# Decoder layer in fp32: a shared product behind the gates, and weight chunks summed on GpSimd ahead of their means

## Chip, core and metric

The kernel runs on one core of a Trainium2 chip. The metric is device time in microseconds (us) of one execution. The texts call the engines by their names and the profile by its short forms: TensorE is PE (PEld is its weight load), VectorE is DVE, ScalarE is ACT, GpSimd is POOL, and SP issues the DMA transfers. A line number such as L997 is a line of the kernel before.

## What is computed

The input x has 16 sequences of 256 tokens of 512 features, all in fp32. Three parts follow each other, each with a residual and a layer norm:

```python
x = _layernorm(x + _L0_attn_ref(x, ...))        # gated state space block
x = _layernorm(x + _L0_xattn_ref(x, k, fside_S2_0, ctx_2048, ctx_2048, 8))
x = _layernorm(x + _L0_ffn_ref(x, W, b, lora_A, lora_B, gate_w, gate_b))
```

The first part projects x to z, xi, dt, B and C, convolves xi over four tokens, scans 16 states per head, and projects back. The second is a long convolution: the 256 rows of each half of the batch are taken as 32 heads of 8 rows; `kv` is the product of every row of v with every row of x2 in a head, it is convolved along the 512 features with the causal kernel of the head, `skip` times `kv` is added, and the result is multiplied with x1 and summed over the rows:

```python
kv = vr[:, :, :, None, :] * x2r[:, :, None, :, :]
y = irfft(rfft(kv, n=2 * L) * rfft(k, n=2 * L)[None, :, None, None, :], n=2 * L)[..., :L]
y = y + kv * skip
out = einsum('bhijl,bhil->bhjl', y, x1r)
```

The third is a feed-forward layer with eight low-rank experts, of which the two with the highest gate values are taken:

```python
base = x_flat @ W.T + b
logits = x_flat @ gate_w.T + gate_b
topk_logits, topk_idx = jax.lax.top_k(logits, 2)
gates = jax.nn.softmax(topk_logits, axis=-1)
out = base + lora_update          # gates times lora_B of lora_A of x_flat, for the two experts
```

## The kernel before

The order of instructions is written out by hand: inside `manual_schedule` every engine runs its instructions in the order in which the program emits them, and the framework adds the waits for data and for buffers. A tile pool with `bufs=n` for a tag holds n tiles of that tag at once; the first write to a further tile waits until the last reader of an earlier one is done.

**Part 1** runs from 0 to about 760 us, in eight groups (`g`) of 512 tokens. A group has ten steps (`i`), each a pair of output channels of xi (`x`), z, B or C. A step emits `first_products` (16 matmuls), then `last_products` of the step before (12 matmuls), then the sums of both on VectorE and ScalarE, and for an `x` step the convolution over tokens in `mixed`: channel 2p begins on VectorE (L575), channel 2p + 1 on ScalarE (L573), and three L577 on VectorE follow for each. These results are tiles of the tag `acc`, of which there are six:

```python
acc = p2.tile([P, GB, S], F32, tag="acc", name="acc", bufs=6)
```

`head_means(0)`, at step 6, reads the accumulators of channels 0 to 3, and `head_means(1)`, at step 8, those of channels 4 to 7. Both write `xm` (L588), a PSUM tile of the tag `tr`, of which there are two. The order of a group from the second on is x0, z0, x1, x2, z1, x3, b0, c1, z2, z3; at step i the sums of step i - 1 are finished, so channels 0 and 1 are mixed at step 1, 2 and 3 at step 3, 4 and 5 at step 4, 6 and 7 at step 6.

In group 1 (105.1 to 201.6 us) the weights of part 3 are prepared beside that. At step 2 `with_identity` adds the residual to `w_f` (L518, L520). At step 5 `centred` takes the mean of `w_f` over its 512 rows and subtracts it, at step 6 that of `w_gl`. The mean is a matmul with `share`, a matrix of 1/512, accumulated over the four chunks of 128 rows (L526) into a tile `mw` of the tag `tr`; the subtraction is four VectorE instructions (L530).

**Part 2 and part 3** run together from about 750 us to the end, one head `h` of 32 after the other. A head's `kv` has two halves `q` of 512 columns. Each half goes through `seeded` (L997, L999), `convolve` (L1010 for whole blocks, L1025 for quadrants of the diagonal), and `contract`: `multiplied` (L1060, tile `pr`) and `reduced` (L1070). Two matrices of the convolution's block rows 2 and 3 share a product with the sum of two input blocks. `seeded` makes it once in the PSUM bank of row 3 and ScalarE copies it, with its two half-partitions exchanged, into the bank of row 2; the later matmuls accumulate onto it. The PSUM tiles `y` (two of two banks) have one buffer each, so the product of the second half waits for the first half's `multiplied`, which reads the same banks.

Between the halves TensorE does part 3 of the head before, which is why `ff` is false in head 0: `centre` transposes `o_l` (L1097) and runs the norm's statistics on ScalarE (L1170, L1088) and GpSimd (L1083, L1090, L1091), with `meanwhile` emitted between mean and squares; then come the eight matmuls of the gates and low-rank rows (`gl`, L1262) and three of the four feed-forward blocks (`base`, L1185). The fourth block, the gates' transposition and `lora` come in the first half of the next head. `gates` (L1104 to L1124) is a run of small VectorE instructions on [128, 8] to [128, 8, 8]. GpSimd also makes `t` (L934), `o` (L948, L952), the pair sums `xs` (L981), the differences `Td` (L986) and the skip products `sk` (L917) for the next head. VectorE makes the next head's `kv` in `products` (L155).

After `base`, `store` scales the finished rows on ScalarE (L1147) and sends them to memory through SP.

Of the kernel before, what the change touches and what calls it, by code (L numbers as in the profile page):

```python
# [8 lines left out]
F32 = mybir.dt.float32  # L9
AF = mybir.ActivationFunctionType  # L10
ALU = mybir.AluOpType
# [3 lines left out]
P = 128  # L15
B, S, D = 16, 256, 512
KD = D // P
# [14 lines left out]
NE, R = 8, 16  # L32
HP = P // 2
# [10 lines left out]
SHARED_AT, DIAGONAL_AT = 3, 5  # L44
# [8 lines left out]
ER = NE * R  # L53
# [17 lines left out]
def decoder_kernel(  # L71
# [24 lines left out]
    nc = tc.nc  # L96
# [83 lines left out]
    with ExitStack() as s1:  # L180
# [3 lines left out]
        p2 = s1.enter_context(tc.tile_pool(name="p2", bufs=2))  # L184
# [326 lines left out]
        def with_identity(w):  # L511

            for k, blk in enumerate(BLOCKS_OUT):
                own = w[:, k, blk * P : (blk + 1) * P]
                if blk in SWAPPED_OUT:
                    for a, b in ((0, HP), (HP, 0)):
                        half = own[:, a : a + HP]
                        nc.vector.tensor_tensor(half, half, ident[:, b : b + HP], ALU.add)  # L518
                else:
                    nc.vector.tensor_tensor(own, own, ident, ALU.add)  # L520

        def centred(w, cols):

            ps = ps_t.tile([P, 512], F32, tag="tr", name="mw")
            for kc in range(KD):
                nc.tensor.matmul(  # L526
                    ps[:, 0:cols], share, w[:, kc, :], start=(kc == 0), stop=(kc == KD - 1)
                )
            for kc in range(KD):
                nc.vector.tensor_tensor(w[:, kc, :], w[:, kc, :], ps[:, 0:cols], ALU.subtract)  # L530

# [6 lines left out]
                nc.sync.dma_start(first[sh][bi], r)  # L538

        heads = {}  # L540
        late = []
        for g in range(NG):
            xs = xs_next
            more = g + 1 < NG
# [95 lines left out]
            for i, (kind, p) in enumerate(order):  # L640
                if g == 1 and i == 2:
                    with_identity(w_f)
                if g == 1 and i in (5, 6):
                    centred(*((w_f, D), (w_gl, NE + ER))[i - 5])
                if i == 6:
                    ms = [head_means(0)]
                if g == 0 and i == 0:
                    al, be = first_products(
                        kinds[kind], p, True, None,
                        lambda: begun.append(begin_products(w_xi, order[1][1], False)),  # L650
                    )
                else:
                    al, be = first_products(
                        kinds[kind], p, i % 3 == 0, begun.pop(0) if begun else None
                    )
                if i == 8:
                    ms.append(head_means(1))
                if i == 9:


                    yps = ps_t.tile([P, S], F32, tag="tr", name="yps")
                    for ht in range(HT):
                        for b in range(GB):
                            nc.tensor.matmul(
                                yps[b * HP : (b + 1) * HP],
                                sel[:, ht].rearrange("p q h -> p (q h)"),
                                Bs[ht][:, b * S : (b + 1) * S],
                                start=(ht == 0),
                                stop=(ht == HT - 1),
                            )  # L670
                if before is not None:
                    finish_products()
                to = places(kind, p)
                u = first_sums(al, be, to)
                if i == 8:
                    states(1, stepped(ms[1], spreads[2]), spreads[3])
                if i == 6:
                    ms = [stepped(ms[0], spreads[0])]
                    spreads.append(spread(1, 1))
                if g == 0:  # L680
                    if i == 1:
                        parts = decays()
                    if i == 2:
                        nc.scalar.activation(A, A, AF.Exp)
                        nc.vector.tensor_scalar(A, A, -1.0, None, ALU.mult)
                    if i in (1, 2, 4):
                        next(parts)
                if i == 9:
                    yT = q3.tile([P, S], F32, tag="vn", name="yT", bufs=1)
                    nc.scalar.copy(yT, yps)  # L690
                if before is not None:
                    finish_sums((lambda: next(parts)) if g == 0 and i == 2 else None)
                if g == 0 and i == 3:
                    next(parts)
                if g == 0 and i in later:
                    for n, (w, k) in enumerate(later[i]):
                        ins = weight_sums(nc.gpsimd, w, k)
                        if n == 0:
                            wait_for(ins, mixes[-1])
                if i == 7:  # L700
                    states(0, ms[0], spreads[1])
                if i == 8:
                    outputs(0)
                    outputs(1)
                    if more:
                        rt = to_dram(rms(xs_next))
                    if g == 0:
                        behind = []
                        w_sums = w_o_sums(behind)
                        next(w_sums)  # L710
                before = (kind, p, al, be, u, to)
                if i < 2 and late:
                    normalised(g - 1, late.pop(0))
                if i == 1 and more:
                    xs_next = load_x(g + 1)
# [95 lines left out]
            late = []  # L811
            if more:
# [36 lines left out]
                late = [(1, xs[1]), (3, xs[3])]  # L849
            else:  # L850
                finish_sums()
                gated(1, spread_heads(1))
                for n, t in enumerate((0, 2, 1, 3)):


                    ps = ps_s.tile([P, 512], F32, tag="s", name="s") if n in (0, 3) else bank()
# [44 lines left out]
    with ExitStack() as s2:  # L901
# [64 lines left out]
        def bank_of(y, lb):  # L966
            n = BLOCKS_OUT.index(lb)
            return y[2] if len(y) > 2 and lb == 2 else y[n // 2][:, n % 2, :]
# [23 lines left out]
        def seeded(y, T, xs, q):  # L992

            yc = bank_of(y, 3)
            nc.tensor.matmul(yc, T[:, SHARED_AT, :], xs[:, q], start=True, stop=True)  # L997
            for a, b in ((0, HP), (HP, 0)):
                nc.scalar.copy(bank_of(y, 2)[b : b + HP], yc[a : a + HP])  # L999

        def convolve(y, kv, T, Td, q, between=None, late=False, early=None, ahead=None):

# [142 lines left out]
        def store(h, x3, nb, rs):  # L1145
            res = p2.tile([P, D], F32, tag="res", name="res")
            nc.scalar.activation(res, x3, AF.Identity, bias=nb, scale=rs)  # L1147
            nc.sync.dma_start(out[h * P : (h + 1) * P, :], res)
# [34 lines left out]
        def feed_forward(base, o_l, kcs, first=False):  # L1183
            for kc in kcs:
                nc.tensor.matmul(  # L1185
                    base, o_l[:, kc, :], w_f[:, kc, :], start=(first and kc == kcs[0]), stop=False
                )

        last, done, rest = None, None, None
        for h in range(HX):  # L1190
# [8 lines left out]
            if h:  # L1199
                if nxt:  # L1200
                    v_after = turned_v(vns.pop(0), ps_b, "vp")
                    kvs.append(load_T(h + 1))
                    if h + 2 < HX:
                        vns.append(load_v(h + 2))
                        cTs.append(load_c(h + 2))
                if rest is not None:
                    base, o_r, xa = rest
                    feed_forward(base, o_r, (3,))
                    turned = turned_gates(xa)
                seeded(y, T, xs, 0)  # L1210
                if rest is not None:
                    lora(base, [turned])
            if ff:
# [34 lines left out]

            def meanwhile():
                skips.append(skip_term(cT, ws, behind))  # L1250
                if nxt:
                    seeded(y, T, xs, 1)

            if ff:
                rs = centre(o_l, meanwhile)
# [3 lines left out]
            if ff:  # L1259
                gl = ps_t.tile([P, NE + ER], F32, tag="tr", name="gl")  # L1260
                for kc in range(KD):
                    nc.tensor.matmul(  # L1262
                        gl, o_l[:, kc, :], w_gl[:, kc, :], start=(kc == 0), stop=(kc == KD - 1)
                    )
                base = ps_b.tile([P, D], F32, tag="base", name="base")
                feed_forward(base, o_l, (0, 1, 2) if nxt else (0, 1, 2, 3), True)
            if ready is not None:
                store(*ready)
            if nxt:
                products(v_n, cT_n, kv_n, 1)  # L1270
                more_next = prepared(kv_n, T_n)
                more_next[2](0)
                more_next[3]()
                sk_next = skip_sums(h + 1, kv_n)
                more_next[2](1)
# [164 lines left out]
```

## Time and profile before

| | before |
|---|---|
| Median of 3 runs | 1461.5 us (1461.34 to 1461.96) |
| The profiled execution | 1461.27 us |
| Its span in the profile | 1459.5 us |
| TensorE busy | 1423.8 us |
| VectorE busy | 1185.4 us |
| ScalarE busy | 438.1 us |
| GpSimd busy | 462.4 us |
| Group 1 of part 1 | 105.10 to 201.64, 96.54 us |
| Groups 2 and 3 of part 1 | 91.96 us each |
| One head of part 2 | 21.6 us |

The span runs from the first instruction to the last, and the time of an execution holds some 1.8 us more. A busy time is the union of an engine's instructions; the ends of matmuls are modelled, so matmuls that follow each other closely overlap in the view, and the distance from start to start tells more than a duration. In a line of the page or of the timeline stand the start and the duration in us (timeline) or the busy time and mean duration (page), the engine, the line, the operation, what it writes and reads with partitions and elements, how often, and in brackets how long the engine had been idle and for whom. One fp32 product appears as two MATMUL records.

### The profile page before, as it was taken

How to read it: one execution, taken by the hardware profiler on the slowest of the kernel's cores; microseconds unless marked ns; L12 is line 12 of the kernel's file. 1: busy time of each engine (PE TensorE's matmuls, PEld its weight loads, DVE VectorE, ACT ScalarE, POOL GpSimd, SP SyncE). 2: the span in 40 equal slices, each digit the busy share in tenths (PEclk: the TensorE clock that was granted, in tenths of full speed). 3: DMA queues.
4: the chain of work that ended last, by engine and by line, in shares of the span. 5: the costliest groups of instructions: out<-in, count | busy, mean ns of one | idle time of the engine just before them, and what ended most of it. 6: DMA issues, size and time to landing. Idle time of an engine off the chain costs nothing.

```text
span 1459.5 us, 19028 instructions
## 1 busy us (share of the span) xinstructions
PE 1423.8 (98%) x6956; PEld 915.1 (63%) x6956; DVE 1185.4 (81%) x2102; ACT 438.1 (30%) x962; POOL 462.4 (32%) x655
## 2 busy tenths in 40 slices
PE   9999999999999999999999999999999999999997
PEld 7788888888888878888773444444443444444443
DVE  6988778787787877878758888888888888888886
ACT  3423223233233332332202232332332333233222
POOL 5450020100101001010015545545554554554552
PEclk9999999999999999999999999999999999999999
DMA  8013111121111212112022122122112212212200
GB/s 294 32 41 125 43 47 44 37 81 31 58 44 36 82 22 69 44 37 89 8 83 65 44 66 73 48 69 65 61 55 66 70 46 66 72 44 65 73 26 22
DMA packets 49166, 89.18 MB, mean 61 GB/s; under 512 B 8880, under 2 KB 13360, under 8 KB 49072
## 3 DMA queue, kind: packets, MB, share of 16 engines
q1 hardware_dynamic: 49072, 87.96, 19.0%
q8 instruction: 55, 0.90, 0.3%
q14 instruction: 39, 0.32, 0.1%
HBM read 70.62 MB, written 17.32 MB: 60 GB/s over the span
## 4 chain that ended last, share of the span: by engine, by line
PE 94%; DVE 4%; issue 1%; POOL 1%; DMA 0%; ACT 0%; POOLq 0%; SPq 0%; DVEq 0%; ACTq 0%
PE mm L328 20%; PE y L1010 15%; PE s L328 13%; PE y L1025 12%; PE base L1185 7%; PE s L768 6%; PE mm L768 6%; PE y L997 4%; DVE pr L1060 3%; PE gl L1262 2%; PE base L1181 2%; PE tr L145 1%; PE mm L725 1%; PE xm L588 1%; PE mm L859 1%
## 5 line engine op out<-in xcount | busy, mean ns | idle before, releaser
L1060 DVE TENSOR_TENSOR pr<-y,cT 128x1024 f32<-128x1024 f32 x126 | 148.5, 1219 | 103.1 <-PE y L1025 103.1
L1025 PE MATMUL y<-kv 64*64 64x512 f32 x1536 | 179.6, 598 | 0.0
L577 DVE SCALAR_TENSOR_TENSOR acc<-xi,wc,acc 128x512 f32<-128x512 f32 x192 | 141.9, 753 | 7.4 <-ACT acc L573 1.7
L1070 DVE TENSOR_REDUCE red<-pr 128x128 f32<-128x1024 f32 x126 | 147.1, 1209 | 0.0
L155 DVE TENSOR_TENSOR kv<-tr,cT 128x1024 f32<-128x1024 f32 x124 | 145.5, 1215 | 0.0
L1010 PE MATMUL y<-kv 128*128 128x512 f32 x272 | 128.2, 594 | 0.6 <-ACT y L999 0.4
L1025 PEld LDWEIGHTS y<-kv 64*64 64x64 f32 x1536 | 52.2, 132 | 119.0 <-issue 96.8
L1185 PE MATMUL base<-w_f,ol 128*128 128x512 f32 x248 | 116.5, 593 | 0.0
L1010 PE MATMUL y<-kv,Td 128*128 128x512 f32 x248 | 116.5, 592 | 0.0
L66 POOL TENSOR_TENSOR rs_a<-ve_a,nhalf 128x1 f32<-128x1 f32 x32 | 18.9, 592 | 242.4 <-DVE ve_a L64 242.4
L1010 PEld LDWEIGHTS y<-kv 128*128 128x128 f32 x272 | 51.1, 190 | 66.4 <-issue 48.9
L997 PE MATMUL y<-xs,kv 128*128 128x512 f32 x124 | 67.9, 629 | 24.5 <-DVE pr L1060 23.5
L389 POOL TENSOR_TENSOR rstd<-ms,nhalf 128x4 f32<-128x4 f32 (+1 forms) x9 | 8.5, 945 | 260.8 <-DVE ms L387 260.8
L328 PE MATMUL mm<-XT,w_z 128*128 128x256 f32 x384 | 90.7, 379 | 0.0
L999 ACT COPY y<-y 64x512 f32<-64x512 f32 x124 | 69.2, 558 | 65.1 <-PE y L997 63.1
L1010 PEld LDWEIGHTS y<-kv,Td 128*128 128x128 f32 x248 | 47.1, 190 | 59.3 <-issue 59.3
L1217 POOL TENSOR_TENSOR ol<-o,red 128x512 f32<-128x512 f32 x31 | 39.4, 1271 | 140.3 <-DVE red L1070 140.3
L981 POOL TENSOR_TENSOR xs<-kv 128x512 f32<-128x512 f32 x63 | 80.0, 1269 | 2.4
L328 PEld LDWEIGHTS mm<-XT,w_z 128*128 128x128 f32 x384 | 73.0, 190 | 9.9
L328 PE MATMUL mm<-xnT,w_z 128*128 128x256 f32 x288 | 71.0, 382 | 0.0
L1185 PEld LDWEIGHTS base<-w_f,ol 128*128 128x128 f32 x248 | 42.5, 190 | 30.9 <-issue 30.9
L328 PE MATMUL s<-XT,w_xi 128*128 128x256 f32 x256 | 61.0, 380 | 0.9 <-DVE XT L224 0.6
(276 smaller groups left out, 2790.9 us busy)
## 6 DMA issues: line engine op xcount, KB each, us to landing
cT<-in_ctxT SPq DMA_DIRECT2D x32, 384.0 KB
kv<-in_toep SPq DMA_DIRECT2D x32, 384.0 KB
xt<-in_x SPq DMA_DIRECT2D x32, 256.0 KB
spread<-both SPq DMA_DIRECT2D x32, 256.0 KB
first<-xt SPq DMA_DIRECT2D x32, 256.0 KB
vn<-first SPq DMA_DIRECT2D x32, 256.0 KB
out<-res SPq DMA_DIRECT2D x31, 256.0 KB
xnT<-in_xT SPq DMA_DIRECT2D x7, 1024.0 KB
```

The lines of the kernel that those rows point to most:

```text
L155: last = nc.vector.tensor_tensor(kv[:, q, k * BQ : (k + NL // 2) * BQ], vT[:, q, blks].rearrange("p k (b i) -> p (k b) i", i=NH).unsqueeze ...
L328: nc.tensor.matmul(ps, w[:, p, a, kc, :], Xs[b][:, kc, :], start=start and kc == 0, stop=stop and kc == 1, skip_group_check=upon,)
L577: ins = nc.vector.scalar_tensor_tensor(acc, xi[:, :, k : k + S], wc[:, c, k : k + 1], acc, ALU.mult, ALU.add)
L768: nc.tensor.matmul(ps, own[a][c][:, n * P : (n + 1) * P], w_o[b][c], start=start and c == 0, stop=stop and c == HC - 1, skip_group_check=upon,
L981: return nc.gpsimd.tensor_tensor(xs[:, q], moving(kv, q, 0), moving(kv, q, 1), ALU.add)
L997: nc.tensor.matmul(yc, T[:, SHARED_AT, :], xs[:, q], start=True, stop=True)
L999: nc.scalar.copy(bank_of(y, 2)[b : b + HP], yc[a : a + HP])
L1010: nc.tensor.matmul(bank_of(y, lb), w, moving(kv, q, mb), start=not late and lb not in begun, stop=False, skip_group_check=True,)
L1025: return nc.tensor.matmul(bank_of(y, lb)[cols], T[rows, DIAGONAL_AT, (b - a) * HP : (b - a + 1) * HP], moving(kv, q, lb)[rows], start=star ...
L1060: nc.vector.tensor_tensor(pr.rearrange("p (k b j) i -> p k b j i", k=2, j=NH), y[i].rearrange("p k (b j i) -> p k b j i", j=NH, i=NH), cT[ ...
L1070: nc.vector.tensor_reduce(red[:, q, 2 * i : 2 * i + 2, :].rearrange("p k t -> p (k t)"), pr, AX.X, ALU.add)
L1185: nc.tensor.matmul(base, o_l[:, kc, :], w_f[:, kc, :], start=(first and kc == kcs[0]), stop=False)
```

## The change

In part 1 the four chunks of `w_f` and of `w_gl` are summed into one tile by three GpSimd additions each (`chunk_sum`, at steps 3 and 4 of group 1), and `centred`, still at steps 5 and 6, takes one product of `share` with that sum instead of four. The sums are tiles of the tag `acc`, with six buffers as before.

In part 2 `seeded` is split: it keeps the product, and `spread_seed` has the two ScalarE copies. In the first half of a head both stay where they were. In the second half the product is no longer emitted in `meanwhile` but behind the gates' matmuls and the first feed-forward block, and the copies come behind the other feed-forward blocks and `store`.

```diff
-        def centred(w, cols):
+        def chunk_sum(w, cols):
+
+            total = p2.tile([P, D], F32, tag="acc", name="w_sum", bufs=6)[:, 0:cols]
+            nc.gpsimd.tensor_tensor(total, w[:, 0, :], w[:, 1, :], ALU.add)
+            for kc in range(2, KD):
+                nc.gpsimd.tensor_tensor(total, total, w[:, kc, :], ALU.add)
+            return total
+
+        def centred(w, cols, total):
 
             ps = ps_t.tile([P, 512], F32, tag="tr", name="mw")
-            for kc in range(KD):
-                nc.tensor.matmul(
-                    ps[:, 0:cols], share, w[:, kc, :], start=(kc == 0), stop=(kc == KD - 1)
-                )
+            nc.tensor.matmul(ps[:, 0:cols], share, total, start=True, stop=True)
             for kc in range(KD):
                 nc.vector.tensor_tensor(w[:, kc, :], w[:, kc, :], ps[:, 0:cols], ALU.subtract)
...
-        late = []
+        late, sums = [], []
...
+                if g == 1 and i in (3, 4):
+                    w, cols = ((w_f, D), (w_gl, NE + ER))[i - 3]
+                    total = chunk_sum(w, cols)
                 if g == 1 and i in (5, 6):
-                    centred(*((w_f, D), (w_gl, NE + ER))[i - 5])
+                    centred(*sums.pop(0))
+                if g == 1 and i in (3, 4):
+                    sums.append((w, cols, total))
                 if i == 6:
                     ms = [head_means(0)]
...
-            yc = bank_of(y, 3)
-            nc.tensor.matmul(yc, T[:, SHARED_AT, :], xs[:, q], start=True, stop=True)
+            nc.tensor.matmul(bank_of(y, 3), T[:, SHARED_AT, :], xs[:, q], start=True, stop=True)
+
+        def spread_seed(y):
             for a, b in ((0, HP), (HP, 0)):
-                nc.scalar.copy(bank_of(y, 2)[b : b + HP], yc[a : a + HP])
+                nc.scalar.copy(bank_of(y, 2)[b : b + HP], bank_of(y, 3)[a : a + HP])
...
                 seeded(y, T, xs, 0)
+                spread_seed(y)
                 if rest is not None:
                     lora(base, [turned])
...
             def meanwhile():
                 skips.append(skip_term(cT, ws, behind))
-                if nxt:
-                    seeded(y, T, xs, 1)
...
-                feed_forward(base, o_l, (0, 1, 2) if nxt else (0, 1, 2, 3), True)
+                feed_forward(base, o_l, (0,), True)
+            if nxt:
+                seeded(y, T, xs, 1)
+            if ff:
+                feed_forward(base, o_l, (1, 2) if nxt else (1, 2, 3))
             if ready is not None:
                 store(*ready)
+            if nxt:
+                spread_seed(y)
             if nxt:
                 products(v_n, cT_n, kv_n, 1)
```

## Prediction

> **What bounds the kernel now.** First the page, for the busy shares and the one group of matmuls that waits:
>
> ```profile
> PE 1423.8 (98%) x6956; PEld 915.1 (63%) x6956; DVE 1185.4 (81%) x2102; ACT 438.1 (30%) x962; POOL 462.4 (32%) x655
> ...
> L997 PE MATMUL y<-xs,kv 128*128 128x512 f32 x124 | 67.9, 629 | 24.5 <-DVE pr L1060 23.5
> ```
>
> TensorE sets the end, and nearly all the idle time that other engines cause it stands before L997, the shared product of `seeded`. The waits of TensorE between 771 and 1423 us show where: 30 waits of at most 0.7 us for `pr` L1060, together 21.8. One head of part 2, TensorE alone in the timeline:
>
> ```profile
> 1064.18 0.66 PE L1097 MATMUL tr<-ident,ol 128*128 128x128 f32 x4
> 1065.57 1.12 PE L997 MATMUL y<-xs,kv 128*128 128x512 f32 x2 [0.72 <-DVE pr L1060]
> 1066.53 1.09 PE L1262 MATMUL gl<-w_gl,ol 128*128 128x136 f32 x8
> 1067.46 2.74 PE L1185 MATMUL base<-w_f,ol 128*128 128x512 f32 x6
> 1070.03 0.59 PE L1010 MATMUL y<-kv 128*128 128x512 f32 x1
> ```
>
> The second transposition group of the same head (L145) needs 0.49 us until the next matmul begins; here L997 begins 1.39 after the transposes, so 0.90 is lost. L997 and L1262 stand 0.96 apart where L1185's pairs take 0.86: another 0.10 from the late weights. The gates (`gl`) and L1185 wait behind L997 though `ol` is complete 3 us earlier. A head, by the windows view:
>
> ```profile
> 1048.60:1070.19 21.59, 20.87 (x96) 8.95 (x96) 18.12 (x26) 6.75 (x16) 11.19 (x17) 1.00 0.18 61
> ```
>
> VectorE has 18.12 of 21.59 us to do. Its slack is 1.35 us before the first `pr` of a head and 1.87 before the second. What it does ahead of the second matters:
>
> ```profile
> 1049.81 0.56 DVE L1113 TENSOR_TENSOR cmp<-lg 128x64 f32<-128x64 f32 x1
> 1050.30 0.21 DVE L1114 TENSOR_TENSOR cmp<-lg 128x64 f32<-128x64 f32 x1
> 1050.43 1.28 DVE L1115 TENSOR_TENSOR cmp<-cmp,tri 128x64 f32<-128x64 f32 x1
> ```
>
> ```profile
> 1050.37 1.26 POOL L981 TENSOR_TENSOR xs<-kv 128x512 f32<-128x512 f32 x1
> 1051.59 0.72 POOL L986 TENSOR_TENSOR Td<-kv 128x256 f32<-128x256 f32 x1
> ```
>
> Three comparisons of one size take 0.56, 0.21 and 1.28: L1113 ends 0.08 after the GpSimd instruction beside it (L952, to 1050.29), L1115 0.08 after L981. `gates` is already held up by GpSimd.
>
> **The Trainium skill.** "TensorE: Matmul & The Clock Gate", Step-by-step: only weight loads are pulled ahead, matmuls stay in program order; the trace agrees (ready `gl` behind L997). The same page, Architectural detail: ScalarE and VectorE are strict FIFO; nothing here contradicts it, and step 2 of part 1 rests on it. "GPSIMD Engine Reference", Specifications: GpSimd shares its SBUF interfaces with VectorE, with contention for instructions with two SBUF inputs; the lines above agree.
>
> **Part 2, TensorE.** In 30 heads (`ff` and `nxt`: h = 1 to 30) `gl` (0.93) and one block of L1185 (0.86) go ahead of L997. t counts from the start of the first `pr` (1064.29). Before: transposes -0.10, L997 1.28, `gl` 2.24, blocks 3.17, convolution 5.74, its end 12.01. After: transposes -0.10, `gl` 0.39, block 0 1.32, L997 2.17, blocks 1 and 2 3.03, convolution 4.75, end 11.02. L997's bank is free at 1.28, 0.9 before it is wanted; so 0.99 per head, 29.7 for 30, is gained if nothing else comes late. Head 0 has no feed-forward block, so its wait of 1.7 us stays. No work is added.
>
> **Part 2, ScalarE.** The two copies (L999) move behind the squares (L1088) and the store's scaling (L1147). Those now start at t = 1.62 instead of 3.62; squares and accumulator 0.78, scaling 0.80, to 3.10. L997 is readable 1.16 after its start, at 3.33; copies to 4.48. The matmul that first needs them is the second of the convolution, at 4.75 + 0.86 = 5.6: 1.1 us of cover, cost nothing; uncovered, the excess per head. The store's DMA is issued 1.9 us earlier on SP with no transfer added; load order there is unchanged. Cost nothing.
>
> **Part 2, GpSimd and VectorE.** What is late next? GpSimd's `var_b` waits for ScalarE's squares (1.85 in this head). They end earlier, so `var_b` follows `t` (L934, ends 2.63), at about 2.70 instead of 4.48: the stream `rs_b`, `o`, `xs`, `Td`, `sk`, `xs` comes 1.78 earlier. `xs` then runs 5.90 to 7.17, `Td` to 7.85, `sk` to 9.29, `xs` to 10.52. VectorE's L1113 is still at 7.12, after products which don't move. Now no pause lets it through: L1113 waits for `xs` (7.25), L1114 for `Td` (7.98, with 0.05 that each holds the other), L1115 for `sk` (9.46), L1117 to 9.78, L1119 for the second `xs` (10.73), and 0.59 more to the end of L1124: 11.3, where it was 10.25. `pr` could start at 11.12 and starts at 11.2. The next head's L997 has no spare time (`pr` frees its bank at 1056.08, it starts at 1056.16), so some 0.05 of 0.99 is given back. I take 0.93 x 30 = **27.9 us** off.
>
> That is close: if `xs` ends before 7.12 (0.05 earlier), L1113 falls to `Td` (7.81), L1114 to `sk` (9.28), L1115 to the second `xs` (10.58), and the gates end at 11.8. `pr` is 0.6 late, and 0.42 x 30 = 12.6 us remain. The 0.07 that I put between `t` and `var_b` is the pause behind L948 and L952; behind L981 and L986 the next begins 0.04 before the end. I take the pause, as `t` has the same kind of four-dimensional operands.
>
> **Part 1, matmuls.** `mw` for `w_f` falls from 8 matmuls (132.79 to 136.22, 3.43) to 2 (0.86), for `w_gl` from 8 (1.02) to 2 (0.26): 3.33 us less, in one group only. Six GpSimd sums are added: three of 128x512 at 1.27 and three of 128x136 at some 0.46 (between 0.72 for 256 columns and 1.27 for 512), with pauses 5.5 us, from 123.6 (`with_identity` done) to 129.1; TensorE wants the first at 132.8. GpSimd has nothing from 122.0 to 166.2, so nothing queues behind them. VectorE's L575 (128.46) and L577 lose at most 0.3, absorbed below.
>
> **Part 1, buffers.** The sums take `acc` tiles, of which there are six. At step 4 the accumulators of channels 0 to 3 live until `head_means(0)` at step 6; two sums live to steps 5 and 6; channels 4 and 5 make eight. Channel 4 gets the buffer of `w_f`'s sum (free by 133.9, wanted 135.43: no wait). Channel 5 gets that of `w_gl`'s sum, free only after its mean at step 6. Before:
>
> ```profile
> 135.54 0.72 ACT L573 ACTIVATE acc<-xi,wc 128x512 f32<-128x512 f32 x1 [1.34 <-DVE xi L372]
> ...
> 140.42 2.48 DVE L530 TENSOR_TENSOR w_f<-w_f,mw 128x512 f32<-128x512 f32 x4
> ...
> 142.26 1.09 PE L526 MATMUL mw<-w_gl,share 128*128 128x136 f32 x8
> 143.28 0.64 PE L588 MATMUL xm<-acc,mean 128*32 128x512 f32 x4
> ```
>
> After: TensorE reaches `w_gl`'s mean at 132.79 + 0.86 + 6.02 = 139.7, done 140.1; then L573 (0.72) to 140.9, three L577 (0.76) to 143.2, four L530 to 145.6. On VectorE L530 stands behind L577; `xm` needs the PSUM buffer that L530 frees. So L588 starts at 145.7 instead of 143.28: **2.4 us lost**, not 3.3 gained. If the buffers are given in another way and nothing waits, VectorE, full from 126.5 to 145.7, lets some 3.0 through; those are the ends, -3.0 and +2.4, and I take +2.4. The later steps follow TensorE.
>
> **Sum.** 1461.27 (profiled execution: span 1459.5 and 1.77 around it) - 27.9 + 2.4 = 1435.8; the median is 0.2 higher: **1436 us**.
>
> **Rivals.** A, forecast: 1436, 0.42. B, as A but no wait for a buffer: 1461.5 - 27.9 - 3.0 = 1430.6, 0.15. For it: TensorE's own order is free to run on; against: the count of eight. C, GpSimd passes the comparisons one boundary earlier: 1461.5 - 12.6 + 2.4 = 1451 (1446 without the buffer wait), 0.33. For it: only 0.05 us of margin. D, the gain isn't there (L997 waits for something that the trace hides behind `pr`): about 1461 to 1464, 0.03. E, slower: GpSimd's stream moves up by only 0.5, not 1.78, because the squares or `t` are late. Then `xs` ends at 8.45, L1113 at 8.5, L1114 at 9.2, L1115 at 10.8, L1119 after 12.0, the gates at 12.6; `pr` 1.4 late gives 0.38 x 30 = 11 lost, and 2.4: 1475. It decides once `xs` ends after about 8.1, a move of under 0.8; against it, the squares wait for nothing but `nm_b`, ready at t = 1.59. 0.07.
>
> Range: A, B and C with 1 to 2 us for sizes, 1429.5 to 1451.5. About 0.2% is what a measurement here can tell from no change: faster 0.90, same 0.03, slower 0.07.
>
> **What would show it.** L997's idle time for `pr` falls from 23.5 to below 4, with `gl` ahead of it; heads come every 20.7 us in A, 21.2 in C; L1113, L1114, L1115 each end just after a GpSimd instruction; L526 has 2 + 2 matmuls; L588's first starts near 145.7 with a wait for L530, L573 waits some 4 us. Wrong if heads stay at 21.6, if TensorE itself stands at L1010 for L999, or if L588 begins by 141.

## The result, and the profile after

The changed kernel takes 1436.36 us in the median of 4 runs (1435.19 to 1437.24), the kernel before 1461.42 (1461.11 to 1461.96). The ratio is 0.9828, with a 95% interval from 0.9811 to 0.9845. The profiled execution took 1436.9 us, with a span of 1435.1.

In the page of the kernel after, the shared product is L1006 (it was L997). Its idle time has fallen from 24.5 us to 2.6, and 2.4 of what is left stands at the beginning of part 2, at 771.7 and 781.0 us:

```profile
PE 1415.7 (99%) x6944; PEld 914.7 (64%) x6944; DVE 1209.7 (84%) x2102; ACT 438.1 (31%) x962; POOL 470.6 (33%) x661
...
L1006 PE MATMUL y<-xs,kv 128*128 128x512 f32 x124 | 64.8, 604 | 2.6 <-DVE pr L1071 1.6
```

TensorE in one head after, by the timeline, shows `gl` (L1272) and the first pair of the feed-forward blocks (L1196) where the idle time was, and not one wait in brackets:

```profile
1036.08 0.65 PE L1108 MATMUL tr<-ident,ol 128*128 128x128 f32 x4
1036.57 1.09 PE L1272 MATMUL gl<-w_gl,ol 128*128 128x136 f32 x8
1037.50 1.02 PE L1196 MATMUL base<-w_f,ol 128*128 128x512 f32 x2
1038.36 1.02 PE L1006 MATMUL y<-xs,kv 128*128 128x512 f32 x2
1039.22 1.88 PE L1196 MATMUL base<-w_f,ol 128*128 128x512 f32 x4
1040.93 0.59 PE L1021 MATMUL y<-kv 128*128 128x512 f32 x1
```

From the transposes to the convolution it is 4.85 us; it was 5.85 (1064.18 to 1070.03).

A group of part 1 is measured from the first matmul of its output product to that of the next group. The spans of the two profiled executions then divide as follows (us):

| stretch | before | after | difference |
|---|---|---|---|
| up to the first output product | 79.45 | 80.41 | +0.96 |
| group 1 | 96.55 | 101.06 | +4.51 |
| groups 2 to 7 | 551.76 | 551.76 | 0.0 |
| the rest: part 2 and the end | 731.7 | 701.9 | -29.8 |

The first row lay between 79.4 and 80.6 in all profiles of this study. No edit has an instruction in that stretch, and kernels with the same part 1 differ there by up to 0.8, so it is not put down to the change. Part 2 gave 29.8 us, and part 1 took 4.5 back. The waits of TensorE between 100 and 205 us have one line, a wait that isn't in the kernel before (L593 was L588, L535 was L530):

```profile
PE xm L593 <- DVE w_f L535: 5.6, 1, 5.6
```

### The profile page after: what moved, and what is told of

Read it like the earlier page. It is cut to its first block, busy times and chain, and to the rows that moved or that the text cites. A ratio compares the mean times of both kernels' runs of the same rounds, so it can differ in the third digit from the quotient of the medians.

```text
span 1435.1 us, 19011 instructions
## 1 busy us (share of the span) xinstructions
PE 1415.7 (99%) x6944; PEld 914.7 (64%) x6944; DVE 1209.7 (84%) x2102; ACT 438.1 (31%) x962; POOL 470.6 (33%) x661
## 4 chain that ended last, share of the span: by engine, by line
PE 96%; DVE 2%; issue 1%; POOL 1%; DMA 0%; ACT 0%; POOLq 0%; SPq 0%; DVEq 0%
PE mm L328 20%; PE y L1021 15%; PE s L328 14%; PE y L1036 12%; PE base L1196 7%; PE s L778 6%; PE mm L778 6%; PE y L1006 4%; PE gl L1272 2%; PE base L1192 2%; PE tr L1108 1%; PE tr L145 1%; PE xm L593 1%; PE mm L735 1%; PE mm L869 1%; PE s L869 1%
## 5 line engine op out<-in xcount | busy, mean ns | idle before, releaser
L1196 PE MATMUL base<-w_f,ol 128*128 128x512 f32 x248 | 121.4, 593 | 0.0
L1006 PE MATMUL y<-xs,kv 128*128 128x512 f32 x124 | 64.8, 604 | 2.6 <-DVE pr L1071 1.6
L1196 PEld LDWEIGHTS base<-w_f,ol 128*128 128x128 f32 x248 | 42.5, 190 | 30.9 <-issue 30.9
```

What stands on the lines that cost most here:

```text
L1006: nc.tensor.matmul(bank_of(y, 3), T[:, SHARED_AT, :], xs[:, q], start=True, stop=True)
L1196: nc.tensor.matmul(base, o_l[:, kc, :], w_f[:, kc, :], start=(first and kc == kcs[0]), stop=False)
```

## The experiments

All ran against the kernel before, whose median was between 1461.4 and 1461.9 us.

**part2_only** has the move of the product and of the copies, and the weights' means as before. Against the changed kernel, in part:

```diff
...
-            nc.tensor.matmul(ps[:, 0:cols], share, total, start=True, stop=True)
+            for kc in range(KD):
+                nc.tensor.matmul(
+                    ps[:, 0:cols], share, w[:, kc, :], start=(kc == 0), stop=(kc == KD - 1)
+                )
...
```

> The means of the weights as in the kernel before (four products each, no GpSimd sums); the move of the shared product and of its copies as in the change. Theory: all the gain is here, 0.99 us in each of 30 heads, so 1461.4 - 29.7 = 1431.7 us, below the changed kernel by the 4.6 that part 1 loses. Rival (the size on record, 0.93 per head, with part 1 losing less): 1433.5. Rival (part 1 gains): above 1436.4.

Measured: 1432.0 us, ratio 0.9797 (0.9783 to 0.9810). Group 1 takes 96.54 us again and the rest 702.0. The whole gain comes from part 2, 0.99 us per head: heads come every 20.604 us, where it was 21.596, and 30 times 0.99 is the 29.7 that the rest has lost.

**part1_only** is the kernel before with `chunk_sum` and the single products, in part:

```diff
...
+                if g == 1 and i in (3, 4):
+                    w, cols = ((w_f, D), (w_gl, NE + ER))[i - 3]
+                    total = chunk_sum(w, cols)
                 if g == 1 and i in (5, 6):
-                    centred(*((w_f, D), (w_gl, NE + ER))[i - 5])
+                    centred(*sums.pop(0))
...
```

> The GpSimd sums and single products for the means as in the change; part 2 as in the kernel before. Theory: TensorE stands 5.6 us for the PSUM buffer of the first mean, net 2.4 after what the fewer matmuls save, and its granted clock falls for some 4 us behind that idle time, about 2.2 more: 1461.4 + 4.6 = 1466.0. Rival (the wait alone, the clock dip belongs to something else): 1463.8. Rival (no buffer wait): 1458.4.

Measured: 1466.43 us, ratio 1.0030 (1.0018 to 1.0041). Part 1's edit alone makes the kernel slower; group 1 takes 101.15 us, and TensorE waits 5.6 us for L535, as in the changed kernel.

**kept_busy** is the changed kernel with matmuls that nobody needs, behind the second mean:

```diff
             nc.tensor.matmul(ps[:, 0:cols], share, total, start=True, stop=True)
+            if cols < D:
+                for _ in range(22):
+                    nc.tensor.matmul(ps[:, 256 : 256 + P], ident, ident, start=True, stop=True)
```

> The change with 22 matmuls of ident added behind the second mean, into unused columns of its PSUM tile; they fill about 4.7 of the 5.6 us in which TensorE stands there. Theory (the idle time lowers the granted clock afterwards): the wait still ends at the same moment, the head means take 1.0 instead of 1.9 us, and the time falls by about 2.2 to 1434.2. Rival (those matmuls are slow for another reason): 1436.4, or more by whatever of the 4.7 doesn't fit.

Measured: 1433.89 us (1433.72 to 1434.19), 2.5 below the changed kernel. In the windows view the stretch and its length are followed by the busy times of PE, PEld, DVE, ACT and POOL, then by the granted clock (1.00 is full speed), the DMA share and its rate. The changed kernel first:

```profile
140.00:148.00 8.00, 2.44 (x14) 0.95 (x12) 6.04 (x11) 2.41 (x5) 0.00 (x0) 0.77 0.00 0
148.00:153.40 5.40, 5.40 (x21) 4.18 (x18) 1.61 (x7) 1.33 (x3) 0.00 (x0) 0.71 0.00 0
153.40:160.00 6.60, 6.60 (x33) 5.80 (x31) 5.31 (x11) 1.48 (x3) 0.00 (x0) 1.00 0.13 40
```

And the same stretches of kept_busy:

```profile
140.00:148.00 8.00, 7.34 (x61) 6.19 (x60) 6.83 (x15) 3.06 (x7) 0.00 (x0) 1.00 0.00 0
148.00:153.40 5.40, 5.40 (x27) 4.75 (x26) 2.60 (x8) 1.07 (x3) 0.00 (x0) 1.00 0.00 0
```

With work in the wait the clock stays at 1.00, the head means follow in 1.00 us instead of 1.87 (start to start of the next matmul), and group 1 takes 98.90 instead of 101.06. So 2.16 of the 4.51 us were the clock behind the idle time, and 2.35 the wait itself. In stretches of half a microsecond, the trace of the changed kernel has the clock at 0.50 from 144.3 us, some 3.2 after the last matmul ahead of the wait, to 151.1; for 4.5 of these 6.8 us TensorE was at work again.

**own_sum_tile** is the changed kernel with seven tiles for six buffers instead of eight:

```diff
-            total = p2.tile([P, D], F32, tag="acc", name="w_sum", bufs=6)[:, 0:cols]
+            if cols < D:
+                total = p2.tile([P, cols], F32, tag="w_sum", name="w_sum", bufs=1)
+            else:
+                total = p2.tile([P, D], F32, tag="acc", name="w_sum", bufs=6)
```

> The change with one edit: the sum of w_gl has a tile of its own (136 columns) instead of one of the six accumulator buffers. Theory (eight tiles want six buffers): with seven tiles for six buffers channel 5 gets the buffer of the first sum, free at 134, L578 starts near 136.6 without waiting for the second mean, TensorE doesn't stand before the head means, the clock stays full, and part 1 gains some 3: 1431.7 - 3.0 = 1428.7. Rival (the loss is GpSimd's sums holding VectorE): no change, 1436.4. Rival (PSUM buffers of the means are too few in any case): about 1434.

Measured: 1433.61 us (1432.57 to 1434.59). The theory's number missed; that of the second rival, about 1434, held. Channel 5 no longer waits for the second mean: its first instruction on ScalarE starts at 137.04. But TensorE still stands before the head means:

```profile
140.88 0.40 PE L536 MATMUL mw<-w_sum,share 128*128 128x136 f32 x2
144.38 1.06 PE L596 MATMUL xm<-acc,mean 128*32 128x512 f32 x8 [3.11 <-DVE w_f L538]
```

VectorE reaches the subtraction (L538) at 141.85, behind the accumulators that stand ahead of it in its order, and `xm` needs the PSUM buffer that it frees. What the six fewer products of `w_f` and of `w_gl` save is waited away: group 1 takes 96.45 us, within 0.1 of the kernel before. In the profiled execution the clock stayed at 1.00 behind this wait of 3.1 us. That execution, at 1432.57 us, is the fastest of the four and 0.5 above part2_only's, and its first stretch is 0.6 longer. The other three took 1433.53 to 1434.59, with a mean granted clock of 0.997 to 0.998 where the profiled one has 0.999. So in them the clock may have fallen behind the same wait; they have no trace, and this is not shown.

**later_second_mean** is own_sum_tile with the mean of `w_gl` one step later, behind the head means:

```diff
-                if g == 1 and i in (5, 6):
+                if g == 1 and i in (5, 7):
                     centred(*sums.pop(0))
```

> The change with the sum of w_gl in a tile of its own and its mean at step 7 instead of 6, so that the head means find the other PSUM buffer free. Theory (what eats the fewer matmuls is the PSUM buffer that the first subtraction frees late): TensorE doesn't stand at the head means, group 1 is some 3.2 shorter than in the kernel before, 1432.0 - 3.2 = 1428.8. Rival (VectorE, full in those steps, stops TensorE one step later): 1432.

Measured: 1429.05 us, ratio 0.9777 (0.9764 to 0.9791), the fastest of all. The head means take the PSUM buffer that the second mean had taken, and TensorE no longer waits in group 1. Around the head means:

```profile
139.67 1.03 PE L328 MATMUL mm<-XT,w_z 128*128 128x256 f32 x4
140.63 1.06 PE L596 MATMUL xm<-acc,mean 128*32 128x512 f32 x8
141.63 1.13 PE L328 MATMUL s<-xnT,w_bc 128*128 128x256 f32 x4
```

Group 1 takes 93.27 us, 3.28 less than before, where the products taken away had taken 3.33. The shortage of PSUM buffers was thus what held own_sum_tile back, and VectorE has room for the rest.

The next four have part 1 as before and are compared with part2_only (1432.0). As in the prediction, t counts from the start of a head's first `pr`. **gates_only_ahead** puts only the gates ahead of the product:

```diff
-                feed_forward(base, o_l, (0,), True)
             if nxt:
                 seeded(y, T, xs, 1)
             if ff:
-                feed_forward(base, o_l, (1, 2) if nxt else (1, 2, 3))
+                feed_forward(base, o_l, (0, 1, 2) if nxt else (0, 1, 2, 3), True)
```

> Part 1 as before; in part 2 only the gates' matmuls go ahead of the shared product, the first feed-forward block stays behind it; the copies as in the change. Theory (0.90 us had to be filled and the bank is free 1.28 after the first multiplication starts): the product would be wanted at 1.32, so nothing or little is lost, 0 to 0.15 per head: 1432 to 1436.5. Rival (the block is what makes the gain safe): TensorE stands 0.3 or more per head, 1441 and up.

Measured: 1433.95 us (1433.47 to 1434.32), heads every 20.667, 0.06 more than in part2_only. The product no longer waits for `pr` here either; the 0.06 stands between the product and the block behind it, 0.92 where such pairs take 0.86. So the gates alone fill almost all of the idle time, and putting the block ahead too gives the last 0.06.

**copies_ahead** emits `gl`, block 0, the product and the copies inside `meanwhile`, so that ScalarE keeps its old order:

```diff
             def meanwhile():
                 skips.append(skip_term(cT, ws, behind))
+                if ff:
...
+                    feed_forward(base, o_l, (0,), True)
+                if nxt:
+                    seeded(y, T, xs, 1)
+                    spread_seed(y)
...
```

> Part 1 as before; TensorE's order in part 2 as in the change, but the copies stay ahead of the squares on ScalarE as in the kernel before (gates, block 0, product and copies are all emitted between the mean and the squares). Theory: the squares end 2.6 later, GpSimd's stream too, so the gates' comparisons meet L952's counterpart instead of xs and end at 10.4 instead of 11.2; nothing else needs the earlier rs: 1432, the copies' move is worth nothing. Rival (the later rs or xs stops VectorE or TensorE): 1440 or more.

Measured: 1431.96 us (1431.60 to 1432.41). That the copies went behind the squares and the store is worth nothing. It even costs room: with the copies ahead, `var_b` starts at t = 5.27 and the gates end at 10.37, well before `pr` is wanted at 11.12, while in part2_only and in the changed kernel they end at 11.2, just in time.

**delayed_gpsimd** puts a small instruction ahead of `var_b`:

```diff
+            if tag == "b":
+                dl = p2.tile([P, 1], F32, tag="dl", name="dl")
+                nc.gpsimd.tensor_scalar(dl, nhalf[:, 0:1], 1.0, None, ALU.mult)
             nc.gpsimd.tensor_scalar(var, var, 1.0 / D, LN_EPS, ALU.mult, ALU.add)
```

> Part 1 as before, part 2 as in the change, with one more GpSimd instruction on a column of 128 values (0.19 and a pause of 0.08) between t and var_b in each of 31 heads. Theory (the gates end at 11.20 in the head, and pr could start at 11.12, so VectorE has nothing to spare): some 0.27 per head late, 30 x 0.27 = 8, so 1440 (1438 to 1443). Rival: GpSimd isn't on the path, 1432.

Measured: 1434.96 us (1434.56 to 1435.27), +3.0 where 8 were expected. The added instruction starts 0.03 before `t` ends, so `var_b` moves by only 0.18 us, from t = 2.70 to 2.88. The gates then end at 11.31 instead of 11.20, and heads come every 20.705 us, 0.10 more each. GpSimd is on the path, but less of the delay arrives than was counted.

**swapped_gpsimd** exchanges two instructions and adds none:

```diff
-                more_next[2](0)
                 more_next[3]()
+                more_next[2](0)
```

> Part 1 as before, part 2 as in the change, and GpSimd makes Td before the first xs instead of behind it: no work added. Theory (each comparison of the gates waits for the GpSimd instruction that runs beside it): the first comparison now waits for xs, the second for sk, the third for the second xs; the gates end 0.75 later, pr with them, and the next head's shared product stands: 30 x 0.75 = 22, so 1454. Rival (VectorE has slack there): 1432.

Measured: 1449.42 us (1449.25 to 1449.48), 17.4 above part2_only. The timeline of GpSimd in one head:

```profile
1044.15 0.73 POOL L986 TENSOR_TENSOR Td<-kv 128x256 f32<-128x256 f32 x1
1044.83 1.27 POOL L981 TENSOR_TENSOR xs<-kv 128x512 f32<-128x512 f32 x1
1046.06 1.48 POOL L917 TENSOR_TENSOR sk<-kv,skip_bc 128x512 f32<-128x512 f32 x1
1047.49 1.28 POOL L981 TENSOR_TENSOR xs<-kv 128x512 f32<-128x512 f32 x1
```

And of VectorE:

```profile
1045.36 0.82 DVE L1114 TENSOR_TENSOR cmp<-lg 128x64 f32<-128x64 f32 x1
1046.11 1.51 DVE L1115 TENSOR_TENSOR cmp<-lg 128x64 f32<-128x64 f32 x1
1047.54 1.30 DVE L1116 TENSOR_TENSOR cmp<-cmp,tri 128x64 f32<-128x64 f32 x1
```

Each comparison, which took 0.21 us undisturbed in the kernel before (L1114), ends 0.08 after the GpSimd instruction beside it. The gates end at t = 11.79, `pr` starts at 11.71 instead of 11.12, and heads come every 21.18 us: 0.58 more, times 30 is 17.4. The 22 expected had the end at 11.95. In the prediction's rival C, too, the last two comparisons stood beside `sk` and the second `xs`, and `pr` was 0.6 late: there because `xs` ended early, here because `xs` and `Td` are exchanged.

## Why the prediction came out right, point by point

**TensorE's order in part 2: right.** The product starts at t = 2.18 (2.17 on record), the convolution at 4.75, and no wait is left for `pr`.

**GpSimd's stream and the comparisons: each step right to about 0.1 us.** In the kernel after, `var_b` starts at t = 2.70, and a pause of 0.08 (0.07 on record) is there behind `t`. `xs` ends at 7.18, 0.06 after the first comparison begins. GpSimd in that head:

```profile
1042.09 1.27 POOL L991 TENSOR_TENSOR xs<-kv 128x512 f32<-128x512 f32 x1
1043.32 0.78 POOL L996 TENSOR_TENSOR Td<-kv 128x256 f32<-128x256 f32 x1
1044.06 1.48 POOL L927 TENSOR_TENSOR sk<-kv,skip_bc 128x512 f32<-128x512 f32 x1
```

VectorE beside it:

```profile
1043.30 0.22 DVE L1124 TENSOR_TENSOR cmp<-lg 128x64 f32<-128x64 f32 x1
1043.43 0.75 DVE L1125 TENSOR_TENSOR cmp<-lg 128x64 f32<-128x64 f32 x1
1044.10 1.52 DVE L1126 TENSOR_TENSOR cmp<-cmp,tri 128x64 f32<-128x64 f32 x1
```

The first comparison passes almost at once, the second ends 0.08 after `Td`, the third 0.08 after `sk` (1045.54). That agrees with the Trainium skill, "GPSIMD Engine Reference", Specifications, which has GpSimd and VectorE share their SBUF interfaces and contend where a VectorE instruction has two SBUF inputs.

**The mis-sized term of part 2:** "so some 0.05 of 0.99 is given back". Nothing was given back. The gates end at 11.20, and `pr` starts at 11.12, 0.08 ahead of the end of the instruction before it (VectorE's instructions overlap by about as much elsewhere in this trace), just when TensorE has its input ready. The prediction let `pr` wait for that end. So 27.9 should have been 29.7 or 29.8. The 27.9 also holds a slip: 0.99 less 0.05 is 0.94, and 0.93 was taken. There is no margin behind `pr`, as delayed_gpsimd shows.

**The wait in part 1: right.** "L588 starts at 145.7": L593 starts at 146.59, which is 145.63 when the 0.96 of the first stretch is taken off. (The 0.46 us for a sum of 136 columns was called "between" the times for 256 and 512 columns; it lies below both, and 0.47 was measured.) ScalarE shows the cause, behind the second mean:

```profile
141.07 0.72 ACT L578 ACTIVATE acc<-xi,wc 128x512 f32<-128x512 f32 x1 [5.65 <-PE mw L533]
141.70 0.35 ACT L357 COPY u<-mm 128x256 f32<-128x256 f32 x1
```

**The term that was missing in part 1:** "2.4 us lost". The wait cost 2.35, but it left TensorE idle for 5.56 us, in which the granted clock fell to 0.50. It stayed there for 4.5 us after the wait, which cost 2.16 more. The step that failed is "The later steps follow TensorE": they followed it at half the clock. The Trainium skill has it ("TensorE: Matmul & The Clock Gate", HAM oscillation: idle gaps of more than about 3.4 us lead to a throttled restart); the profiled executions agree, with a dip in 5.56 us of idle time and none in 3.11. No run here measures the limit itself, and the other executions of own_sum_tile leave open whether 3.11 us is always short enough.

**Rival B was mis-sized too:** without the wait for a buffer VectorE does not "let some 3.0 through". In own_sum_tile next to nothing comes through (0.1), because the head means still wait for the PSUM buffer. Only later_second_mean, where that buffer is free too, gains 3.28. Against this rival the prediction set only the count of eight `acc` tiles, and not the two PSUM buffers.

The two misses of the forecast, 1.9 us too little gained and 2.1 too little lost, cancel. That the 1436 on record lies within 0.4 of the measured 1436.36 is luck: the mechanisms were right, and two sizes were not.

## What to carry to other kernels

When an engine waits in its own order, look for what is ready behind the waiting instruction, then ask which engine has to be on time next, to a tenth of a microsecond. Work taken off the bounding engine is a gain only if the buffers that it passes through come free as early; count the tiles that live at once, in SBUF and in PSUM, before adding one. An idle stretch of TensorE can have a price beyond its length: here 5.56 us of it lowered the clock and cost 2.16 us more.

## What was unexpected of the hardware

Matmuls that compute nothing of use made the kernel 2.5 us faster (kept_busy), because they kept the granted clock at 1.00 through a wait. And the order of two independent GpSimd instructions of 1.27 and 0.73 us was worth 17.4 us over 30 heads (swapped_gpsimd), through three small VectorE instructions that happen to run beside them.
